# Turning a graph's mask rows with DMA transposes instead of TensorE products

## The chip, the core and the metric

The kernel runs on one core of a Trainium2 chip. The metric is the time of one execution on the device in microseconds (us). The engines are named as in the profile: PE is TensorE (PEld its weight loads), DVE is VectorE, ACT is ScalarE, POOL is GpSimd, SP is SyncE. An engine works through its own list of instructions in order, and that list is fixed when the kernel is built. DMAs are issued from the lists of SP, ACT and POOL.

## The reference

Four graph layers run one behind the other on x (2708 x 512, f32), all with the same 0/1 neighbour matrix adj (2708 x 2708, int32; symmetric pattern with the diagonal set, some 2% ones). Only the first two concern us; layers 2 and 3 are attention layers, which use the same mask.

```python
# layer 0: at most the first 64 neighbours of each row are kept
Ab   = A > 0
keep = Ab & (cumsum(Ab, axis=1) <= 64)
cnt  = keep.sum(axis=1, keepdims=True)
xj   = leaky_relu((keep @ X / max(cnt, 1)) @ W_nb.T + b_nb)
xi   = leaky_relu(X @ W_line.T + b_line)
x    = layernorm(x + xi + where(cnt > 0, xj, 0))
# layer 1: all neighbours
agg  = (adj > 0) @ x / max(deg, 1)
comb = concat([x @ W_self + b_self, agg @ W_nb + b_nb])
x    = layernorm(x + relu(comb @ W_comb + b_comb))
```

## The kernel before

**Tiles.** The 2708 rows are 22 tiles (`NT`) of 128 rows (`P`); the last has 20 (`few`). `maskT` holds the turned mask in SBUF for the whole kernel, one byte an element: `maskT[p, j, n]` belongs to neighbour `j * 128 + p` of row `n`. A neighbour that is among the first 64 has another sign in it than one that comes later, so that layer 0 gets its mask with a Relu of the negated value, and layer 1 by asking for what isn't zero.

**How one mask tile is made.** `turns` lists the tiles in the order in which the mask is made: 20, 21, then 0 to 19; "mask i" below is the i-th of this list. Four steps belong to each.

- `load_mask` (L272): one DMA on POOL's queue reads 128 rows of adj and converts int32 to bf16 on the way into a tile `m` (or `spare`, `w`).
- `count` (L277): ACT turns the row into 0/1 and adds up the degree.
- `place` (L283, L286): DVE runs a scan along the row, which numbers the neighbours, and multiplies the row with it, in two parts (stage 1) or four (stage 2). After this the sign of an element tells whether it is kept.
- `turn` (L295, L299, L302): 22 PE products with an identity write the 128 x 128 blocks turned into PSUM, eight blocks to a bank; ACT's Sign brings each bank to `maskT` as fp8; a small DMA on POOL's queue makes a second copy of the last 20 neighbours' rows on partitions 32 to 51.

**Stage 1 (to about 207 us).** A loop over the 22 tiles of x. For each: `xTs` turns the next x tile on PE (L133, L135); one product with W_nb (L259), whose result `keep_y` stores as a high part by ACT (`yH`, L231) and a low part by DVE (`yL`, L236); one product with W_line (L259), to which DVE adds the bias (`u`, L352) and applies the leaky function (L195); POOL stores that to `r0_dram` (L354). SP loads the x rows (L173) into three buffers, two tiles ahead. The first 14 masks (`HERE`) are made between these steps, at most one per tile: at tile 2, 3 and so on, with two tiles on the way left without one. A mask is turned two tiles after it was counted (one for the last), and there are three buffers `m`, so one mask is loaded while one is counted and placed and one waits for its turn.

**Stage 2 (207 to about 479 us).** `keep @ (X W_nb.T)` for six blocks of up to four row tiles, the blocks in the order of `turns`: for each block, 22 steps over neighbour tiles `j`. A step makes `kT` from maskT on ACT (L369) and runs up to eight matmuls (L496), a high and a low part for each of four row tiles. Each step also asks a generator `both` for one piece of other work: first `other_masks` (masks 14 to 21, in buffers `spare` and `w` by turns), then `weights1` (products of layer 1's weight matrices, one of which it leaves in `weight2`), then `vectors` (24 steps on DVE, L479 and L480, with a load each). What is left of the 132 steps' worth is done at the end. `finish` (L414 to L421) ends layer 0 for the block before. The pools of stage 1 and stage 2 (`l0a`, `l0b`) lie on the same memory, so that stage 2's buffers become free when stage 1's are no longer read.

**Order.** `pe` chains PE's instructions of stage 1 by hand, in the order of the program. `tc.issue_after(ins)` puts the instructions of a block behind `ins` on its engine. Everything else is ordered by the framework's planner when the kernel is built: it goes by the order of the program and by its own estimate of when an instruction's inputs are there, and it waits for a buffer until all uses of the old content are done.

Of the kernel before, what the change touches and what calls it, by code (L numbers as in the profile page):

```python
# [11 lines left out]
BF16 = mybir.dt.bfloat16  # L12
F8 = mybir.dt.float8e4
AF = mybir.ActivationFunctionType
# [4 lines left out]
P = 128  # L19
# [7 lines left out]
STEP = 2.0 ** 68  # L27
# [3 lines left out]
def kernel(  # L31
# [9 lines left out]
    nc = tc.nc  # L41
    N = x.shape[0]
    NT = -(-N // P)
    FULL = N // P
# [5 lines left out]
    def rows(t):  # L50
        return min(P, N - t * P)
# [11 lines left out]
    identb = const.tile([P, P], BF16, name="identb")  # L63
    nc.vector.tensor_copy(identb, ident)
    G = 8
# [16 lines left out]
    maskT = big.tile([P, NT, NT * P], F8, name="maskT")  # L82
# [12 lines left out]
    few = N - (NT - 1) * P  # L95
    LAST, TWIN = NT - 1, 32
# [61 lines left out]
    def early(first, n, make):  # L158

        made = {}  # L160

        def get(i, **how):
            for j in range(len(made), min(i + first + 1, n)):
                made[j] = make(j, **how)
            return made[i]
        return get
# [36 lines left out]
    with ExitStack() as phase:  # L203
        yp = phase.enter_context(tc.tile_pool(name="y", bufs=1))
        cnts = yp.tile([P, NT], F32, name="cnts")
# [3 lines left out]
        gate = yp.tile([P, 1], F32, name="gate")  # L209
        nc.vector.memset(gate, -STEP / 2)  # L210
        weight2 = yp.tile([P, KD, D], F32, name="weight2")
# [6 lines left out]
        ps_mm = phase.enter_context(tc.tile_pool(name="ps_mm", bufs=1, space=PSUM))  # L218
        ps_a = phase.enter_context(tc.tile_pool(name="ps_a", bufs=4, space=PSUM))
        sums = lambda dtype=F32, shape=(P, D): ps_a.tile(list(shape), dtype, name="acc", tag="acc")  # L220
# [44 lines left out]
        HERE = NT - 8  # L265
        cuts = [(b, min(b + 4, NT)) for b in range(0, NT, 4)]
        cuts = cuts[-1:] + cuts[:-1]
        turns = [t for b in cuts for t in range(*b)]

        def load_mask(i, m):  # L270
            n = rows(turns[i])
            nc.gpsimd.dma_start(m[:n], adj[turns[i] * P:turns[i] * P + n, :], max_dma_last_dim=N * 2)  # L272
            return m

        def count(i, m):
            t, n = turns[i], rows(turns[i])
            nc.scalar.activation(m[:n], m[:n], AF.Sigmoid, bias=gate[:n], scale=STEP, accum_out=cnts[:n, t:t + 1])  # L277

        def place(i, m, places, part, of):

            n = rows(turns[i])
            c0, c1 = N * part // of, N * (part + 1) // of
            nc.vector.tensor_tensor_scan(places[:n, :c1 - c0], m[:n, c0:c1], over[:n].to_broadcast([n, c1 - c0]),  # L283
                                         places[:n, c0 - N * (part - 1) // of - 1:][:, :1] if part else -KEEP - 0.5,
                                         OP.add, OP.min)
            return nc.vector.tensor_mul(m[:n, c0:c1], m[:n, c0:c1], places[:n, :c1 - c0])  # L286

        def turn(i, m, psum, order=as_it_comes):
            t, n = turns[i], rows(turns[i])
            for g0 in range(0, NT, G):  # L290
                g1 = min(g0 + G, NT)
                ps = psum()
                for j in range(g0, g1):
                    w = rows(j)
                    order(nc.tensor.transpose(ps[:w, j - g0, :n], m[:n, j * P:j * P + w], identb[:n, :n]))  # L295
                parts = [(P, g0, min(g1, FULL))] + ([(rows(FULL), FULL, NT)] if g1 > FULL else [])
                for w, a, b in parts:
                    if a < b:
                        nc.scalar.activation(maskT[:w, a:b, t * P:t * P + n], ps[:w, a - g0:b - g0, :n], AF.Sign,  # L299
                                             saturate=False)  # L300
                if g1 == NT:
                    nc.gpsimd.dma_start(maskT[TWIN:TWIN + few, LAST, t * P:t * P + n],  # L302
                                        maskT[:few, LAST, t * P:t * P + n])
                yield

        def rows_of(src):
            return early(2, NT, lambda t: fetched(src, t, rows(t)))

        with ExitStack() as ph:
            st = ph.enter_context(tc.tile_pool(name="l0a", bufs=1))  # L310
            wnT, wlT = weight(), weight2
            room = [maskT[:, G + k, :4 * D].bitcast(F32) for k in range(2 * KD)]

            xs = rows_of(x)
            xTs = early(0, NT, lambda t, order=as_it_comes: transposed(ahead, ps_tr, xs(t), rows(t), "xT", order))

            transpose_weight(room[:KD], ps_tr, wnT, l0_w_nb, (nc.sync, nc.scalar))
            lows = {}  # L320
            for t in range(2):
                xT = xTs(t, order=pe)
                lows[t] = keep_y(t, P, product(xT, P, wnT, 0, pe))
            transpose_weight(room[KD:], ps_tr, wlT, l0_w_line)
            b_line = bias(bcast(l0_b_line, D))
            masks = early(1, HERE, lambda i: load_mask(i, st.tile([P, N], BF16, name="m", bufs=3)))
            masks(0)
            nc.gpsimd.memset(maskT[:, NT - 1, :], 0.0)
            nc.gpsimd.memset(maskT[:, :, N:], 0.0)
            counted = turned = 0  # L330
            for t in range(NT):
                n = rows(t)
                if t > 1:

                    lows[t] = keep_y(t, n, product(xTs(t, order=pe), n, wnT, 0, pe, sums() if t % 2 else None))
                xT = xTs(t)
                if t + 1 < NT:
                    xTs(t + 1, order=pe)
                while turned < counted - (t + 2 < NT):
                    for _ in turn(turned, masks(turned), lambda: sums(BF16, (P, G, P)), pe):  # L340
                        pass
                    turned += 1
                now = counted < min(HERE, -(-(t - 1) * HERE // (NT - 5)))
                if now:
                    m, places = masks(counted), st.tile([P, N // 2], BF16, name="places", bufs=1)
                    with tc.issue_after(highs[t].ins):
                        count(counted, m)
                    with tc.issue_after(lows[t].ins):
                        place(counted, m, places, 0, 2)
                pm = product(xT, n, wlT, 1, pe)  # L350
                u = sm.tile([P, D], F32, name="u")
                nc.vector.tensor_add(u[:n], pm[:n], b_line[:n])  # L352
                low = rows_made = leaky(u[:n], u[:n])
                nc.gpsimd.dma_start(r0_dram[t * P:t * P + n, :], u[:n])  # L354
                if now:
                    with tc.issue_after(low.ins):
                        place(counted, m, places, 1, 2)
                    counted += 1
# [3 lines left out]
        with ExitStack() as ph:  # L362
            st = ph.enter_context(tc.tile_pool(name="l0b", bufs=1))
# [8 lines left out]
            def other_masks():  # L372

                def room(i):
                    r = (ahead.tile([P, 2 * KD * (D + 2 * H)], BF16, name="w", tag="w", bufs=1) if i % 2 else
                         st.tile([P, 2 * KD * D], BF16, name="spare", tag="spare"))
                    m = r[:, :N]
                    load_mask(i, m)
                    return m, r[:, N:N + N // 4 + 1]

                got = {HERE: room(HERE)}
                for i in range(HERE, NT):
                    if i + 1 < NT:
                        got[i + 1] = room(i + 1)
                    m, places = got.pop(i)
                    if i == HERE:
                        for _ in range(5):
                            yield
                    count(i, m)
                    yield  # L390
                    yield
                    for part in range(4):
                        place(i, m, places, part, 4)
                        yield
                    yield
                    yield
                    psum = (ps_mm.tile([P, G, P], BF16, name=f"pm{k % 2}") for k in range(3))
                    for _ in turn(i, m, lambda: next(psum)):
                        yield
                nc.vector.tensor_scalar(iso, cnts, 0.5, None, op0=OP.is_lt)  # L400
                nc.vector.tensor_scalar(rdeg, cnts, 1.0, None, op0=OP.max)
                nc.vector.reciprocal(rdeg, rdeg)
# [83 lines left out]
            for i, b in enumerate(cuts):  # L486
# [19 lines left out]
                for t in ts_:  # L506
                    n = rows(t)
# [9 lines left out]
            for t in range(NT):  # L517
                n = rows(t)
# [3 lines left out]
                for p in {19: (16, 17), 20: (18, 19), 21: (20, 21)}.get(t, (t - 3,)):  # L522
                    if p >= 0:
                        with tc.issue_after(low.ins):
                            nc.vector.tensor_scalar(maskT[:, p, :], maskT[:, p, :], 0.0, None, op0=OP.not_equal,
                                                    saturate=False)
                if t + 1 < NT:
                    xTs(t + 1)
                pm = product(xT, n, wself, 1)
# [4 lines left out]
        with ExitStack() as ph:  # L534
            st = ph.enter_context(tc.tile_pool(name="l1b", bufs=2))
            for t in range(NT):
                n = rows(t)
# [3 lines left out]
                for g0 in range(0, NT, G):  # L541
                    g1 = min(g0 + G, NT)
# [948 lines left out]
```

## Time and profile before

| | |
|---|---|
| median of 3 runs | 2942.97 us (2942.67 to 2946.18) |
| profiled execution | 2939.28 us, span 2937.5 us, mean granted clock 0.995 |
| PE, DVE, ACT, POOL busy | 97%, 68%, 52%, 7% of the span |
| products with the identity (L295) | 308 in stage 1, 176 in stage 2 |
| Sign from PSUM to maskT (L299) | 56 instructions in stage 1, 32 in stage 2; 1.03 us at the longest |
| loads of mask rows (L272) | 14 in stage 1, 8 in stage 2 |

Lines of the profile give the line of the kernel, the engine, the operation, what it writes and reads, its shapes and how often it occurs; in brackets how long the engine was idle just before, and for whom. In the timeline the first two columns are the start and the time of a group of like instructions, in us. "pm", "acc" and "ps_tr" are PSUM buffers. Numbers at the end of names are left out, so `weight` in the profile is `weight2`.

### The profile page before, as it was taken

The page shows a single profiled execution, that of the slowest core. Times are in us where ns is not written, and L with a number is a line of the kernel's source. Part 1 is how long each engine was busy: PE and PEld are TensorE (multiplying, and loading weights), DVE is VectorE, ACT ScalarE, POOL GpSimd, SP SyncE. Part 2 cuts the span into 40 slices and gives each one's busy share as a digit, 9 for nine tenths or more (in the row PEclk, how much of TensorE's full clock was granted, in tenths as well). Part 3 has the DMA queues.
Part 4 walks back from the last instruction along what each step waited for, and adds up shares of the span by engine and source line. Part 5 has one row for each costly group of instructions (what it writes and reads, how often), then busy time and mean ns, then how long its engine had stood idle before and what let it go on. Part 6 is the DMA issues. An engine that isn't in the chain of part 4 may idle for free. (4 is left out here: it accounts for less than half of the span.)

```text
span 2937.5 us, 36437 instructions
## 1 busy us (share of the span) xinstructions
PE 2854.5 (97%) x14354; PEld 1590.3 (54%) x14354; DVE 1996.9 (68%) x2409; ACT 1515.0 (52%) x1761; POOL 220.2 (7%) x375
## 2 busy tenths in 40 slices
PE   8999999999999999999999999999999999999997
PEld 4557766458887333444466433444475555555555
DVE  6866637443234999999977999999953435445242
ACT  3546532123323999999965999999951000000001
POOL 1111101101110000000022000000000000000000
PEclk9999999999999999999999999999999999999999
DMA  5633326322222011111143111121061000000000
GB/s 131 129 87 76 104 79 192 113 67 91 81 74 82 30 40 39 38 45 48 32 151 123 40 40 39 43 64 37 33 158 61 4 26 15 25 15 16 15 22 21
DMA packets 121886, 185.71 MB, mean 63 GB/s; under 512 B 42455, under 2 KB 67276, under 8 KB 121706
## 3 DMA queue, kind: packets, MB, share of 16 engines
q1 hardware_dynamic: 91838, 121.62, 13.8%
q0 software_dynamic: 18864, 57.45, 6.9%
q10 hardware_dynamic: 11004, 4.22, 0.6%
q8 instruction: 115, 1.88, 0.3%
q14 instruction: 65, 0.53, 0.1%
HBM read 153.10 MB, written 44.65 MB: 67 GB/s over the span
## 5 line engine op out<-in xcount | busy, mean ns | idle before, releaser
L743 DVE SCALAR_TENSOR_TENSOR e<-v_bc,ucol,maskT 128x1408 f32<-128x1408 f32 (+3 forms) x804 | 1135.9, 1468 | 326.9 <-PE pn L1119 313.4
L770 ACT ACTIVATE c<-e,bcol 128x1300 fp8e4<-128x1300 f32 (+1 forms) x688 | 965.5, 1422 | 65.3 <-DVE e L743 22.3
L937 PE MATMUL po<-e,R 128*64 128x512 f32 (+2 forms) x4224 | 907.5, 549 | 30.4 <-DVE e L743 27.4
L937 PEld LDWEIGHTS po<-e,R 128*64 128x64 f32 x4224 | 341.9, 137 | 563.0 <-issue 386.1
L1119 PE MATMUL pn<-e,R 128*128 128x512 f32 (+3 forms) x1056 | 403.0, 545 | 1.1 <-DVE lin L1139 0.3
L1119 PEld LDWEIGHTS pn<-e,R 128*128 128x128 f32 (+1 forms) x1056 | 183.9, 190 | 197.1 <-issue 181.5
L1069 ACT ACTIVATE w<-pl,b 128x256 f32<-128x256 f32 (+1 forms) x88 | 41.0, 466 | 371.2 <-PE pl L1067 371.2
L496 PE MATMUL acc<-yH,kT 128*128 128x512 f32 x484 | 195.2, 409 | 4.6 <-ACT kT L369 4.5
L547 PE MATMUL acc<-yH,mf 128*128 128x512 f32 x484 | 185.0, 389 | 0.0
L496 PE MATMUL acc<-yL,kT 128*128 128x512 f32 x462 | 180.7, 391 | 0.0
L547 PE MATMUL acc<-yL,mf 128*128 128x512 f32 x462 | 179.7, 389 | 0.0
L663 PE MATMUL pm<-w,xT 128*128 128x264 f32 (+1 forms) x704 | 165.3, 387 | 2.0 <-ACT xT L135 1.1
L259 PE MATMUL pm<-weight,xT 128*128 128x512 f32 (+1 forms) x344 | 158.4, 603 | 8.1 <-DVE u L352 6.8
L1067 PE MATMUL pl<-lin 128*128 128x256 f32 (+1 forms) x704 | 156.1, 376 | 3.4 <-DVE lin L966 3.4
L122 POOL TENSOR_TENSOR ln_rs<-ln_rs,half 128x1 f32<-128x1 f32 (+1 forms) x88 | 53.5, 608 | 1407.7 <-DVE ln_rs L121 1358.2
L1092 PE MATMUL pl<-lin,w 128*128 128x512 f32 x336 | 150.8, 593 | 0.0
L1067 PEld LDWEIGHTS pl<-lin 128*128 128x128 f32 x704 | 131.3, 193 | 34.6 <-issue 15.8
L544 ACT CAST mf<-maskT 128x1024 fp32r<-128x1024 fp8e4 (+1 forms) x66 | 64.5, 978 | 151.7 <-PE acc L547 148.1
L663 PEld LDWEIGHTS pm<-w,xT 128*128 128x128 f32 (+1 forms) x704 | 127.9, 187 | 26.2 <-issue 2.9
L259 PE MATMUL pm<-w,xT 128*128 128x512 f32 x296 | 133.6, 594 | 5.3 <-ACT xT L135 2.1
L369 ACT ACTIVATE kT<-maskT 128x512 fp32r<-128x512 fp8e4 (+1 forms) x132 | 77.5, 594 | 115.5 <-PE acc L496 114.3
L839 PE MATMUL pd<-c,parts_c 128*12 128x384 fp8e4 (+2 forms) x2752 | 128.3, 307 | 0.0
(247 smaller groups left out, 2643.2 us busy)
## 6 DMA issues: line engine op xcount, KB each, us to landing
rows<-x_dram SPq DMA_DIRECT2D x63, 256.0 KB
v_bc<-v_dram SPq DMA_DIRECT2D x16, 704.0 KB
rows<-in_x_dram SPq DMA_DIRECT2D x42, 256.0 KB
x_dram<-u POOLq DMA_DIRECT2D x42, 256.0 KB, 2.6
v_bc<-v_dram SPq DMA_DIRECT2D x16, 650.0 KB
m<-in_adj_dram POOLq DMA_DIRECT2D x13, 677.0 KB, 7.0
r_dram<-u POOLq DMA_DIRECT2D x21, 256.0 KB, 2.4
rows<-r_dram SPq DMA_DIRECT2D x21, 256.0 KB
```

The lines of the kernel that those rows point to most:

```text
L259: order(nc.tensor.matmul(pm[:m], xT[:, k, :m], w[:, k, :], start=(k == 0), stop=(k == KD - 1)))
L369: made = nc.scalar.activation(kT[:, :w], maskT[:, j, b[0] * P:b[0] * P + w], AF.Relu, scale=-1.0)
L496: nc.tensor.matmul(pa[t], kT[:, (t - b[0]) * P:(t - b[0] + 1) * P], y[:, j, :], start=(j == 0 and y is yH), stop=(j == LAST))
L547: nc.tensor.matmul(pa, mf[:, j - g0, :], y[:, j, :], start=(j == 0 and y is yH), stop=(j == LAST))
L663: nc.tensor.matmul(pm[a][:m, :D // 2 + heads], xT[:, k, :m], w[:, k, a, :D // 2 + heads], start=(k == 0), stop=(k == KD - 1))
L743: self.made = nc.vector.scalar_tensor_tensor(e[:, :w], v[:, :w], ucol[:, j, h:h + 1], maskT[:, j, c0:c0 + w], op0=OP.max, op1=OP.mult)
L770: nc.scalar.activation(c[:, :w], e[:, :w], AF.Sigmoid, bias=bcol[:, j, h:h + 1], scale=STEP, saturate=False)
L839: pe(nc.tensor.matmul(p[32 * g:32 * g + 12, :c1 - c0], parts_c[:, j, h, :], c[:, c0:c1], start=(i == 0 and h == hs[0]), stop=(i == NT - 1 ...
L937: pe(nc.tensor.matmul(po[i][HO * k:HO * k + HO, :c1 - c0], R2[:, j, h * HO:(h + 1) * HO], e[:, c0:c1], start=(i_ == 0), stop=(i_ == NT - 1)))
L1067: nc.tensor.matmul(pl[:, :w], self.lin1[:, k, f * P:(f + 1) * P], h[:, k, :w], start=(k == 0), stop=(k == KD - 1))
L1092: nc.tensor.matmul(pl[:n], gT[:, f, (t - t0) * P:(t - t0) * P + n], self.lin2[:, f, :], start=(f == 0), stop=(f == KF - 1))
L1119: nc.tensor.matmul(pn[k][:, :w], R2[at, j, k * P:(k + 1) * P], e[at, :w], start=(j == 0), stop=(j == NT - 1))
```

## The change

The 22 products and the PSUM buffers are gone. `turn` is one DMA transpose on SP's queue from the mask tile into a bf16 tile of the turned shape (`turned_` in stage 1, the memory of `weight2` in stage 2). A new generator `signs` has ACT bring that tile to `maskT` in four instructions of 8, 8, 5 and 1 blocks, and then issues the small second copy. `signs` of a mask runs just before the next mask is turned (stage 1), or between the four parts of the next mask's `place` (stage 2).

As the transpose takes whole blocks of 128, a mask tile has 2816 columns instead of 2708; POOL clears the last 108 before each load, and the whole tile where it has only 20 rows. In stage 1 there are two buffers `m` instead of three, besides the one `turned_`. Each mask of stage 2 takes as many steps of `both` as before, and the signs of the last one four more.

```diff
         def load_mask(i, m):
...
-            nc.gpsimd.dma_start(m[:n], adj[turns[i] * P:turns[i] * P + n, :], max_dma_last_dim=N * 2)
+            nc.gpsimd.dma_start(m[:n, :N], adj[turns[i] * P:turns[i] * P + n, :], max_dma_last_dim=N * 2)
...
-        def turn(i, m, psum, order=as_it_comes):
+        def turn(i, m, into):
+            nc.sync.dma_start_transpose(into, m)
+
+        def signs(i, into):
             t, n = turns[i], rows(turns[i])
-            for g0 in range(0, NT, G):
-                g1 = min(g0 + G, NT)
-                ps = psum()
-                for j in range(g0, g1):
-                    w = rows(j)
-                    order(nc.tensor.transpose(ps[:w, j - g0, :n], m[:n, j * P:j * P + w], identb[:n, :n]))
-                parts = [(P, g0, min(g1, FULL))] + ([(rows(FULL), FULL, NT)] if g1 > FULL else [])
-                for w, a, b in parts:
-                    if a < b:
-                        nc.scalar.activation(maskT[:w, a:b, t * P:t * P + n], ps[:w, a - g0:b - g0, :n], AF.Sign,
-                                             saturate=False)
-                if g1 == NT:
-                    nc.gpsimd.dma_start(maskT[TWIN:TWIN + few, LAST, t * P:t * P + n],
-                                        maskT[:few, LAST, t * P:t * P + n])
+            for w, a, b in [(P, a, min(a + G, FULL)) for a in range(0, FULL, G)] + [(few, FULL, NT)]:
+                nc.scalar.activation(maskT[:w, a:b, t * P:t * P + n], into[:w, a:b, :n], AF.Sign, saturate=False)
                 yield
+            nc.gpsimd.dma_start(maskT[TWIN:TWIN + few, LAST, t * P:t * P + n],
+                                maskT[:few, LAST, t * P:t * P + n])
...
-            masks = early(1, HERE, lambda i: load_mask(i, st.tile([P, N], BF16, name="m", bufs=3)))
+            turned_ = st.tile([P, NT, P], BF16, name="turned", bufs=1)
+
+            def mask_rows(i):
+                m = st.tile([P, NT * P], BF16, name="m", bufs=2)
+                nc.gpsimd.memset(m[:, N:], 0.0)
+                if rows(turns[i]) < P:
+                    nc.gpsimd.memset(m, 0.0)
+                return load_mask(i, m)
+
+            masks = early(1, HERE, mask_rows)
...
                 while turned < counted - (t + 2 < NT):
-                    for _ in turn(turned, masks(turned), lambda: sums(BF16, (P, G, P)), pe):
+                    for _ in signs(turned - 1, turned_) if turned else ():
                         pass
+                    turn(turned, masks(turned), turned_)
                     turned += 1
+                if t + 1 == NT:
+                    for _ in signs(turned - 1, turned_):
+                        pass
...
                 def room(i):
...
-                    m = r[:, :N]
+                    m = r[:, :NT * P]
+                    nc.gpsimd.memset(m[:, N:], 0.0)
                     load_mask(i, m)
...
+                into = weight2.rearrange("p k c -> p (k c)").bitcast(BF16)[:, :NT * P].rearrange("p (t n) -> p t n", n=P)
                 for i in range(HERE, NT):
...
                     for part in range(4):
                         place(i, m, places, part, 4)
+                        next(left, None)
                         yield
+                    for _ in left:
+                        pass
                     yield
                     yield
-                    psum = (ps_mm.tile([P, G, P], BF16, name=f"pm{k % 2}") for k in range(3))
-                    for _ in turn(i, m, lambda: next(psum)):
-                        yield
+                    turn(i, m, into)
+                    left = signs(i, into)
+                    yield
+                    yield
+                    yield
+                for _ in left:
+                    yield
```

More of the change, by code (lines that the diff above doesn't have):

```diff
@@ L276, in count @@
             t, n = turns[i], rows(turns[i])
-            nc.scalar.activation(m[:n], m[:n], AF.Sigmoid, bias=gate[:n], scale=STEP, accum_out=cnts[:n, t:t + 1])
+            nc.scalar.activation(m[:n, :N], m[:n, :N], AF.Sigmoid, bias=gate[:n], scale=STEP, accum_out=cnts[:n, t:t + 1])
         def place(i, m, places, part, of):
@@ L376, in room @@
                          st.tile([P, 2 * KD * D], BF16, name="spare", tag="spare"))
-                    m = r[:, :N]
+                    m = r[:, :NT * P]
+                    nc.gpsimd.memset(m[:, N:], 0.0)
                     load_mask(i, m)
-                    return m, r[:, N:N + N // 4 + 1]
-                got = {HERE: room(HERE)}
+                    return m, r[:, NT * P:NT * P + N // 4 + 1]
+                got, left = {HERE: room(HERE)}, iter(())
+                into = weight2.rearrange("p k c -> p (k c)").bitcast(BF16)[:, :NT * P].rearrange("p (t n) -> p t n", n=P)
                 for i in range(HERE, NT):
```

## The prediction

> **What bounds the kernel now.** I read the page first, then the busy times by stretch, then the answer on the products of the old turning (L295), then the timeline of stage 1, then the DMA issues.
>
> ```profile
> span 2937.5 us, 36437 instructions
> PE 2854.5 (97%) x14354; PEld 1590.3 (54%) x14354; DVE 1996.9 (68%) x2409; ACT 1515.0 (52%) x1761; POOL 220.2 (7%) x375
> ```
>
> TensorE is busy 97% of the span, so work taken off it should count, but only where it ends last. The stretches (PE, PEld, DVE, ACT, POOL busy, then clock, DMA share, GB/s) show two kinds of place.
>
> ```profile
> 100.00:150.00 50.00, 48.14 (x204) 24.90 (x203) 45.90 (x43) 28.61 (x40) 8.38 (x14) 1.00 0.60 123
> ...
> 300.00:350.00 50.00, 49.45 (x248) 38.26 (x247) 38.10 (x55) 28.02 (x43) 7.93 (x12) 1.00 0.40 101
> ```
>
> In stage 1 (to 207 us) DVE is nearly as full as PE; in stage 2 (300 to 350) PE alone is the bound. The old turning is in both:
>
> ```profile
> L295 PE MATMUL acc<-identb,m x308: 166/219/230, 50.3 to 195.3; 128*128 128x128 bf16 x143, 20*128 20x20 bf16 x11
> ...
> L295 PE MATMUL pm<-identb,w x88: 219/219/232, 232.4 to 376.1; 128*128 128x128 bf16 x84, 128*20 128x128 bf16 x4
> ```
>
> 308 products turn 14 masks in stage 1; in stage 2 twice 88 (the line shown and its like for the tile spare) turn 8. A product's 219 ns is mostly pipeline: the timeline has 22 begin at 159.03 and the next matmul at 160.45, so 1.42 us a mask, 65 ns a product. One mask in steady state, the lines of masks before and behind it left out:
>
> ```profile
> 117.91 0.72 POOL L272 DMA_DIRECT2D m<-in_adj_dram  x1
> ...
> 125.06 2.55 ACT L277 ACTIVATE m<-m,gate 128x2708 bf16<-128x2708 bf16 x1 [0.43 <-DMA m<-in_adj_dram]
> ...
> 130.97 2.97 DVE L283 TENSOR_TENSOR_SCAN places<-m,over 128x1354 bf16<-128x1354 bf16 x1
> ...
> 139.15 0.86 DVE L286 TENSOR_TENSOR m<-m,places 128x1354 bf16<-128x1354 bf16 x1
> ```
>
> The mask is loaded (7.15 us from issue to use), counted, and placed from 130.97 to 140.0, 9.0 us with three small DVE instructions inside; PE's next product, at 125.93, waits 0.66 us for DVE's u (L352). The next mask's scan comes 9.56 us after this one's: that pace is DVE's, not PE's, whose turn costs 8.83 us with a mask and 7.3 without. The ends of stage 1, and what idling costs PE:
>
> ```profile
> 57.03 0.84 DVE L286 TENSOR_TENSOR m<-m,places 20x1354 bf16<-20x1354 bf16 x1
> ...
> 62.65 5.37 PE L259 MATMUL pm<-weight,xT 128*128 128x512 f32 x8 [2.11 <-DVE u L352]
> ...
> 182.96 0.86 DVE L286 TENSOR_TENSOR m<-m,places 128x1354 bf16<-128x1354 bf16 x1
> ...
> 206.89 0.50 PE L496 MATMUL acc<-yH,kT 128*128 128x512 f32 x1
> ```
>
> Mask 1 is placed at 57.9, mask 13 at 183.8, stage 2 runs from 206.9 (two of its matmuls, 0.5 us, came earlier, so 206.4). The eight matmuls behind a 2.1 us idle took 5.37 instead of 3.70.
>
> Last, prices of transfers, issue to landing in us:
>
> ```profile
> m<-in_adj_dram POOLq DMA_DIRECT2D x13, 677.0 KB, 7.0
> ...
> oT_dram<-oT POOLq DMA_DIRECT2D x4, 704.0 KB, 3.6
> ```
>
> **Part by part.**
>
> *Stage 2, products gone.* 176 x 65 ns = 11.5 us off the engine that bounds it. ACT's signs have the shapes of the old evacuations (1.03, 1.03, 0.72, 0.25 us), read SBUF instead of PSUM, and are taken at the same cost. A mask takes 11 steps as before, about 1.88 us each (eight matmuls 0.235 apart), so the three steps behind the turn and the two behind the count leave some 9 us before the first sign: they hide a DMA up to 9 us. Without that cover ACT would wait with kT behind it and PE behind kT. **-11.5**.
>
> *Stage 1, products gone.* 14 x 1.42 = 20 us of PE, but with masks arriving at DVE's pace most of it only turns into waiting for DVE. It is not counted by itself: the chain below decides the end.
>
> *Two mask buffers instead of three, and the buffer held until the DMA has read it.* This is the new wait. The load of mask i+2 (and the memset before it, on POOL) waits until the transpose of mask i has landed; that waits on SP for mask i's last product with places. So from "mask i placed" to "mask i+2 placed": transpose T, memset 0.3 (128x48 took 0.14, 128x128 f32 0.20, plus hand-over), load 7.0, count 2.7, place 9.0, hand-over to SP 0.2: 19.2 + T. Before, a third buffer covered the load. Queued behind the waiting memset on POOL is a store of r0, whose u tile (two buffers) DVE then needs; behind the waiting transpose on SP are loads of x rows, two tiles ahead; behind a waiting count on ACT the yH copies. Loads now start up to 2.1 us after their buffer is free (117.91 against 115.83, behind such a store); here that would count. Bounds 0 and 2.1 a pair; I take 0.5, as it arises only when the store's turn falls badly.
>
> *T.* The trace has no transpose. It moves 128 x 2816 x 2 B = 704 KB. A plain move of 704 KB lands in 3.6; the mask load, which handles every element since it converts, lands in 7.0 (6.5 to 12.5). A transpose also handles every element, so I take **6**, nearer the latter, and keep 3.6 and 12.5 as ends.
>
> One rule speaks against the change: the Trainium skill, "VectorE: DVE Perf Modes", section "The three transpose paths", lists 390 ns for a 128x128 bf16 transpose on TensorE and 1309 on the DMA, and its "Rules for kernel authors" prefer TensorE where PSUM will do as destination. The 65 ns measured here for one of a row of 22 is far below the page's 390, so that figure overprices what is removed; 22 x 1309 ns would by estimate make T 28.8 and the sum some 160 us larger. The skill's "DMA: Bandwidth & Descriptors", section "Latency and other measured facts", gives 261 GB/s for DMA transposes: by estimate T 2.8, and the sum about -15.
>
> *Sum for stage 1.* Pair: 19.2 + 6 + 0.5 = 25.7. Mask 13 is six pairs behind mask 1: 57.9 + 154.2 = 212.1. Then its transpose 6, signs 2.7, first kT 0.4: 221.2. Stage 2 can't begin before: its buffers lie on those of stage 1 (now mask 14's load waits for mask 13's last product). Products of the x tiles don't depend on masks and should run ahead, done near 206.4 - 20 = 186. So stage 2 starts 14.8 later; PE, idle before, begins slowly, +1.7 (5.37 - 3.70). **+16.5**.
>
> *Tail of stage 2.* other_masks now yields 97 steps, not 93 (four signs of the last mask), so of all 140 the 132 in the blocks leave four more vector steps to the end: 4 x (0.69 + 0.69) = 5.5 us of DVE around 480 to 500, where DVE is full and PE waited 0.4. Between 0 and 5.5; I take **+2**, since only what holds back a yL or u costs.
>
> *Rest.* The full memset of the short mask falls before 10 us and is needed at 42.5: nothing; uncovered it would cost about 2.5 (a memset of 2816 fp8).
>
> Total: -11.5 + 16.5 + 2 = **+7** on the profiled 2939.28 (span 2937.5), 2946.3; the median 2942.97 is 3.7 above that run, so **2950.0**. Each us of T counts seven times: +7 + 7 x (T - 6).
>
> **Rivals.**
>
> *Cheap transpose.* T = 3.6 as the plain move: 7 - 16.8 = -9.8, so 2933. For: same bytes, and the DMA engines are 0.60 busy in the fullest stretch. Against: per-element work. The sign turns at T = 5. A still shorter T gains less and less, as DVE's own work (9.56 a mask) takes over: what can go there are its gaps around the two tiles without a mask, some 6 us, and the 1.4 of turning at tile 20, so stage 1 -7.5, in all about -17, 2926.
>
> *Products don't run ahead.* If queue order keeps tiles 19 to 21 behind mask 13, the 22.6 us from last place to stage 2, less 1.4, come after 212.1: 233.3, +26.9 instead of +14.8, without the slow start: -11.5 + 26.9 + 2 = +17.4, 2960. For: DVE and ACT work in order, counts now wait for loads. Against: the trace has u (L352) set between scan and product where that was ready.
>
> *Long transpose.* Contended as the slowest mask load was: T = 12.5, +52.5, 2995. For: the same 0.60, and POOL's loads, stores and the transposes meet. Against: median 7.0. That the transposes aren't single transfers but fall into small pieces would look the same.
>
> **How the numbers follow.** Forecast 0.34 (T 5 to 7: 2943 to 2957), cheap 0.30, not ahead 0.20, long 0.16. A measurement can tell about 0.2% (5.9 us) from no change. Forecast: 0.14 within, 0.20 slower. Cheap: 0.26 faster, 0.04 within. The others are slower. Faster 0.26, same 0.18, slower 0.56. The range goes from 2926 to 2985 (T near 11), leaving out some of long and what may lie below cheap. Since both signs hold much, the forecast's own range is 2943 to 2957.
>
> **What would show it.** Right: no L295 products; 22 SP transposes landing near 6 us; from mask 2 on, scans in stage 1 some 12.8 us apart; POOL's memset waiting for the transpose; first L496 near 221; PE in stage 2 shorter by 11.5. Wrong: landing under 5 us with scans near 9.6 apart and an earlier stage 2; matmuls of tiles 19 to 21 behind mask 13's place; ACT waiting for the transposes in stage 2 with kT behind, which would give back the 11.5.

## The result: 2955.2 us, 0.4% slower

The changed kernel takes 2955.19 us in the median of 6 runs (2954.36 to 2958.68), the kernel before 2943.66 in the same series (2940.78 to 2946.18): ratio 1.004, 95% interval 1.0027 to 1.0053. The profiled execution took 2954.36 us. The page:

```profile
span 2952.5 us, 35575 instructions
PE 2833.2 (96%) x13870; PEld 1568.3 (53%) x13870; DVE 1997.9 (68%) x2409; ACT 1522.1 (52%) x1761; POOL 261.1 (9%) x398
```

PE has 484 instructions and 21 us of work less than before, and the span is 15.0 us longer. The stretches shown before (PE, PEld, DVE, ACT, POOL busy, clock, DMA share, GB/s):

```profile
100.00:150.00 50.00, 39.43 (x100) 17.83 (x99) 38.93 (x34) 25.85 (x32) 8.55 (x17) 0.92 0.82 166
300.00:350.00 50.00, 48.28 (x205) 37.36 (x205) 40.09 (x63) 31.42 (x48) 10.39 (x17) 1.00 0.62 145
```

In stage 1 PE falls from 48.1 of 50 us to 39.4 and DVE from 45.9 to 38.9: now no engine is full there, so a wait sets the end. In stage 2 (second line) PE is still nearly full. The instructions of the new turning line (L289; min/median/max in ns, first and last start) and who waits for them:

```profile
L289 SPq DMA_TRANSPOSE turned<-m x14: 3283/3386/5587, 50.6 to 214.2; - x14
L289 SPq DMA_TRANSPOSE weight<-spare x4: 3289/3318/3369, 250.9 to 371.1; - x4
...
  POOL m L323: 70.5, 12
  ACT maskT L294: 41.7, 15
```

The 3.4 us (the median) are the time for which a transpose holds SP's list: after the one at 150.53 the next load on SP is issued at 154.00. POOL's memset (L323), and with it the load of the next mask, waits 70.5 us in 12 waits. One cycle of a mask, other lines left out:

```profile
132.28 0.72 POOL L272 DMA_DIRECT2D m<-in_adj_dram  x1 [0.29 <-issue]
...
138.94 2.55 ACT L277 ACTIVATE m<-m,gate 128x2708 bf16<-128x2708 bf16 x1 [4.40 <-DMA m<-in_adj_dram]
...
141.62 2.98 DVE L283 TENSOR_TENSOR_SCAN places<-m,over 128x1354 bf16<-128x1354 bf16 x1 [3.86 <-ACT m L277]
...
149.52 0.85 DVE L286 TENSOR_TENSOR m<-m,places 128x1354 bf16<-128x1354 bf16 x1
...
150.53 3.38 SPq L289 DMA_TRANSPOSE turned<-m  x1
...
157.13 0.19 POOL L323 MEMSET m<- 128x108 bf16 x1 [5.28 <-DMA turned<-m]
```

Load 6.66 us, count 2.68, place 8.75, hand-over 0.16, landing 6.60: 24.85 from the load until the same buffer is cleared again. Two buffers take turns at that, so a mask comes every 12.6 us (mean of the first scans from 66.55 to 205.30) where it was 9.56. The ends of stage 1:

```profile
58.97 0.84 DVE L286 TENSOR_TENSOR m<-m,places 20x1354 bf16<-20x1354 bf16 x1
...
205.30 2.98 DVE L283 TENSOR_TENSOR_SCAN places<-m,over 128x1354 bf16<-128x1354 bf16 x1 [4.04 <-ACT m L277]
...
209.69 3.03 DVE L283 TENSOR_TENSOR_SCAN places<-m,places,over 128x1354 bf16<-128x1354 bf16 x1
...
212.63 0.67 DVE L358 TENSOR_TENSOR u<-pm,bias 128x512 f32<-128x512 f32 x1
213.22 0.85 DVE L286 TENSOR_TENSOR m<-m,places 128x1354 bf16<-128x1354 bf16 x1
...
213.35 3.70 PE L259 MATMUL pm<-weight,xT 128*128 128x512 f32 x8 [1.25 <-DVE u L358]
...
220.77 3.70 PE L259 MATMUL pm<-weight,xT 128*128 128x512 f32 x8
...
226.14 3.64 PE L259 MATMUL acc<-w,xT 128*52 128x512 f32 x8 [1.67 <-POOL xT L257]
...
233.94 0.50 PE L511 MATMUL acc<-yH,kT 128*128 128x512 f32 x1
```

Mask 13 is placed at 214.07. One of PE's eight-matmul products began 0.7 us earlier (213.35), behind u; four more, those of the last two tiles, come only then, and stage 2 starts at 233.94, 27.05 us later than before (206.89). What PE and ACT waited for in stage 1 (us in total, times, longest):

```profile
ACT m L277 <- DMA m<-in_adj_dram: 44.2, 11, 5.5
...
ACT maskT L294 <- DMA turned<-m: 39.6, 14, 8.9
...
PE pm L259 <- DVE u L358: 30.0, 12, 5.7
```

ACT waits 84 us in all for loads and landings, with copies to yH and xT behind these waits in its list; PE waits 30.0 us for u, which before was 5.5.

### The profile page after: what moved, and what is told of

It reads as the page before. It is cut to its first block, busy times and chain, and to the rows that moved or that the text cites. A ratio compares the mean times of both kernels' runs of the same rounds, so it can differ in the third digit from the quotient of the medians.

```text
span 2952.5 us, 35575 instructions
## 1 busy us (share of the span) xinstructions
PE 2833.2 (96%) x13870; PEld 1568.3 (53%) x13870; DVE 1997.9 (68%) x2409; ACT 1522.1 (52%) x1761; POOL 261.1 (9%) x398
## 2 busy tenths in 40 slices
DMA packets 184538, 201.50 MB, mean 68 GB/s; under 512 B 105111, under 2 KB 129932, under 8 KB 184362
## 5 line engine op out<-in xcount | busy, mean ns | idle before, releaser
L1084 ACT ACTIVATE w<-pl,b 128x256 f32<-128x256 f32 (+1 forms) x88 | 41.1, 467 | 369.8 <-PE pl L1082 369.8
L259 PE MATMUL pm<-weight,xT 128*128 128x512 f32 (+1 forms) x344 | 166.3, 629 | 32.1 <-DVE u L358 31.3
```

The source lines that it names most:

```text
L259: order(nc.tensor.matmul(pm[:m], xT[:, k, :m], w[:, k, :], start=(k == 0), stop=(k == KD - 1)))
```

## Experiments

The kernel before took 2941 to 2946 us (medians of 15 to 19 runs) beside these. "Stage 1 ends" below is PE's first matmul of stage 2 in the profile, 202.66 before and 229.71 after (two such matmuls come some 4 us ahead of the rest). These ends have some 2 us of play: the first mask's scan starts at 39.2 to 39.5 us in five of the fourteen profiles (39.30 before) and at 41.1 to 41.8 in nine (41.25 after), whatever was edited.

**The change in stage 2 alone** (stage 1 with three buffers and products as before)

```diff
-                    for _ in signs(turned - 1, turned_) if turned else ():
+                    for _ in turn_pe(turned, masks(turned), lambda: sums(BF16, (P, G, P)), pe):
                         pass
-                    turn(turned, masks(turned), turned_)
...
```

> DMA transposes for the eight masks of stage 2 alone; stage 1 with products and three buffers as in the kernel before. Theory, buffers: stage 2 loses 176 products of 65 ns and nothing waits for the transposes: stage 2 takes 261 us instead of 272.4, the start of layer 1 is 1.4 us shorter as well, time about 2943.7 - 12.8 = 2931 us. Rival, traffic: transposes cost what they bring also here (signs that come late hold kT); time 2940 us or more.

Measured: 2933.23 us, ratio 0.9961 (0.9949 to 0.9973), 11.5 below the kernel before in that series. Stage 1, unchanged, ends at 204.30 in this profile. The eight landings cost next to nothing: PE's idle time for kT is 6.5 us, 4.5 before. The transpose issued at 225.46 clears the way for the next memset at 230.86, 5.4 us later, and five steps of PE's work, some 9 us, hide it.

**The change in stage 1 alone**

```diff
-                    turn(i, m, into)
-                    left = signs(i, into)
-                    yield
-                    yield
-                    yield
+                    psum = (ps_mm.tile([P, G, P], BF16, name=f"pm{k % 2}") for k in range(3))
+                    for _ in turn_pe(i, m, lambda: next(psum)):
+                        yield
```

> DMA transposes for the 14 masks of stage 1 alone, two buffers; stage 2 with products as in the kernel before. Theory, buffers: the whole loss and none of the gain: stage 2 starts near 234 and takes 272 us, time about 2955 + 12.8 = 2968 us. Rival, that part of the loss comes from stage 2 (late masks, more steps at its end): 2960 us or less.

Measured: 2969.61 us, ratio 1.0091 (1.0077 to 1.0105), +24.9; stage 1 ends at 229.60, as with the whole change. The two halves add up: +24.9 and -11.5 make +13.4, the whole is +11.5. All of the loss comes with the change in stage 1.

**Each transpose of stage 1 twice**

```diff
-            nc.sync.dma_start_transpose(into, m)
+            for _ in range(2 if i < HERE else 1):
+                nc.sync.dma_start_transpose(into, m)
```

> Each transpose of stage 1 is issued twice in a row, the same content to the same place; the rest is the changed kernel (2955.2 us). If the time from place to landing (T, 6.5 us) is a term of the chain that sets stage 1, a second transpose lengthens it by at least the 3.4 us for which one held SP, at most by another 6.5: six pairs of masks and the last one make 7 x 3.4 = +24 to 7 x 6.5 = +45, so 2979 to 3000 us. If stage 1 is set by something else (the order of the products, the missing buffer without regard to T), the second transpose fills a queue that otherwise idles: under +8, below 2963 us.

Measured: 3018.36 us, ratio 1.0241 (1.0221 to 1.0261), some 60 us above the changed kernel, with stage 1 ending at 290.98. More than expected, and the profile says why (SP's list, then POOL's):

```profile
115.16 12.28 SPq L290 DMA_TRANSPOSE turned<-m  x2
```

```profile
129.43 0.19 POOL L324 MEMSET m<- 128x108 bf16 x1 [12.98 <-DMA turned<-m]
```

The second transpose writes the same tile as the first and goes 8 to 10 us after it (one pair at 96.42 and 106.13), so a dose is a whole landing, not SP's 3.4 us: from issue to the memset 14.3 us in this pair. From the end of place to the memset it is 16.3 us in the mean of 12 masks, 6.7 in the changed kernel. A pair of masks took 36.0 us instead of 25.2: 9.6 us more landing make 10.8 more per pair. So T is a term of the chain, with a factor of about one per pair, as the prediction's sum had it. The products of the last tiles are done by 248.4 here, while mask 13 is placed only at 277.05: the chain alone sets this end.

**A third mask buffer** (on memory of yL that is written last)

```diff
-                m = st.tile([P, NT * P], BF16, name="m", bufs=2)
+                m = (yp.tile([P, NT * P], BF16, name="m3", tag="late") if i % 3 == 2 else
+                     st.tile([P, NT * P], BF16, name="m", bufs=2))
```

> The changed kernel with three mask buffers in stage 1 (the third on memory that stage 1's low parts need only from tile 18 on). Theory, buffers: the pace of 12.6 us a mask comes from the load of mask i+2 waiting for the transpose of mask i (pair 19.2 + 0.5 + 6 us); a third buffer covers it, so scans come 9.6 us apart as before, stage 2 starts near 206 and the time is about 2955 - 27 = 2928 us. Rival, traffic: the transposes crowd the DMA engines (0.77 busy in stage 1 against 0.51) and slow loads and stores however many buffers there are; then scans stay 12 us or more apart and the time stays above 2948 us.

Measured: 2942.53 us, ratio 0.9991 (0.9981 to 1.0). Between the two theories. Stage 1 ends at 216.21: of stage 1's 27 us the buffer gives 13.5 back. The first masks come 9 to 10 us apart as before, then there are holes (ACT's and PE's lines of the timeline):

```profile
93.92 2.83 ACT L304 ACTIVATE maskT<-turned 128x1024 fp8e4<-128x1024 bf16 x4 [10.88 <-DMA turned<-m]
...
97.74 5.40 PE L269 MATMUL acc<-w,xT 128*128 128x512 f32 x8 [4.30 <-ACT xT L135]
```

This mask's transpose was issued at 82.06, held SP for 7.02 us and landed only after 11.9 (the DMA engines were 0.88 busy from 50 to 90 us, 0.82 in the changed kernel's 100 to 150); ACT's signs waited for it with the next copy to xT behind them. From issue to the memset it is 7.9 us in the mean of 11 masks, 6.6 in the changed kernel. So the missing buffer was half of stage 1's loss, and with it back the landing itself took longer.

**Products ahead: 11 masks in the loop, three after it**

```diff
...
-                now = counted < min(HERE, -(-(t - 1) * HERE // (NT - 5)))
+                now = counted < min(11, -(-(t - 1) * 11 // (NT - 5)))
...
+            while turned < HERE:
+                if counted < HERE:
+                    m, places = masks(counted), st.tile([P, N // 2], BF16, name="places", bufs=1)
+                    count(counted, m)
...
+                turn(turned, masks(turned), turned_)
```

> The changed kernel with 11 masks between the x tiles instead of 14 and the last three after them, so that products of tiles 19 to 21 needn't stand behind mask 13 in the queues. Theory, queue order: two things make stage 1 longer, the pace of the masks (12.6 us) and the three tiles behind the last one (19.9 us from its place to stage 2); here only the first is left, mask 13 is placed near 213 as in the changed kernel, stage 2 starts near 225 instead of 234 and the time is about 2946 us. Rival, pace alone: the planner would have held the products back anyway, stage 2 starts within 3 us of 234, time 2952 to 2958 us.

Measured: 2960.67 us, ratio 1.0054 (1.0042 to 1.0066), missed by both. The products are done by 219, and then:

```profile
225.99 3.75 SPq L289 DMA_TRANSPOSE turned<-m  x1
...
235.02 0.79 PE L521 MATMUL acc<-yH,kT 128*128 128x512 f32 x1 [15.93 <-ACT kT L385]
```

Stage 2 now follows the last transpose by 9.0 us, the 9.1 of the prediction's sum, but that transpose starts at 226.0 instead of 214.2: the first scans come 13.8 us apart in the mean (64.69 to 216.40) where they came 12.6. In the program a mask is counted and placed behind the copies of its x tile, which would make tiles without a mask hold the chain up as masks hold the products; that reading of the 13.8 is argued, not shown. What is shown is that the products, put ahead, leave the masks later.

**Cut transposes** (10 and 12 blocks, the first after the first part of place)

```diff
-            nc.sync.dma_start_transpose(into, m)
+            for a, b in ((0, 10), (10, NT)) if i < HERE else ((0, NT),):
+                nc.sync.dma_start_transpose(into[:, a:b], m[:, a * P:b * P])
```

> Each transpose of stage 1 is cut in two, blocks 0 to 9 and 10 to 21; the first may go after the first part of place, 3.9 us (a scan of 3.0 and a product of 0.85) before the second part is done. The same bytes move, and there are still two buffers. If T is a term of the chain, what follows the second part is 12 of 22 blocks: T falls from 6.5 us to between 3.6 (in proportion) and 4.5, which in six pairs and the last mask is 7 x 2.0 to 7 x 2.9, -14 to -20 us: 2935 to 2941 us. If the traffic of the transposes or the order of the products sets stage 1, nothing comes back: 2952 to 2960 us.

Measured: 2958.24 us, ratio 1.0036 (1.0024 to 1.0049). The premise was half wrong: from the end of place to the memset the mean fell from 6.7 to 5.4 us only (12 masks each). Even these 1.4 us a pair did not arrive, as a pair took 25.5 us (25.2 in the changed kernel), and the time lies in the second theory's range. ACT's waits for landings rose from 39.6 to 62.7 us.

**ACT's order: signs behind the copy of the next x tile** (`copies[0]` is ACT's last copy to xT), with two buffers, and the same with cut transposes

```diff
-                    for _ in signs(turned - 1, turned_) if turned else ():
-                        pass
+                    with tc.issue_after(copies[0].ins):
+                        for _ in signs(turned - 1, turned_) if turned else ():
+                            pass
```

> The changed kernel with its two mask buffers (2955.2 us); only the order of ACT's list is another: in stage 1 the signs of a mask stand behind the copy of the next x tile. If the chain through the two buffers (load, count, place, landing) sets stage 1, ACT's order is beside it: 2951 to 2957 us. If it was ACT's waiting for landings, 39.6 us in 14 waits with copies and counts behind them, that held the products, up to 10 us come back: about 2945 us.

> The transposes of stage 1 cut in two, with two buffers, and the signs behind the copy of the next x tile. Cut alone they gave 2958.2 us, though the place-to-landing time of the second half was 3.8 us in the trace instead of 6.5; ACT then waited 62.7 us in 18 waits for landings, since the signs of the first half came earlier in its list. If that waiting ate the gain, this one has it: 7 x 2.7 = 19 us below 2955, about 2937 us. If a shorter landing gives nothing because DVE and ACT are shared by masks and products (one list each), it stays at 2952 to 2958 us.

Measured: 2968.65 us, ratio 1.0078 (1.0064 to 1.0092); cut as well 2975.94, 1.0101 (1.0085 to 1.0117). Neither theory of either run had slower. The same transfers and buffers, and 11 us more if each is taken against the kernel before in its own series (+22.5 and +11.5). In the profiles stage 1 ends 8.4 us later, at 238.08. The profile of the first:

```profile
110.19 2.55 ACT L277 ACTIVATE m<-m,gate 128x2708 bf16<-128x2708 bf16 x1 [15.38 <-DMA m<-in_adj_dram]
112.74 0.56 ACT L231 CAST yH<-acc 128x512 fp32r<-128x512 f32 x1
...
113.20 0.58 ACT L135 COPY xT<-ps_tr 128x512 f32<-128x512 f32 x1
...
113.84 5.40 PE L259 MATMUL pm<-w,xT 128*128 128x512 f32 x8 [4.51 <-ACT xT L135]
```

A count that waits for its load stands ahead of yH and xT, as in the changed kernel, but here it waits up to 15.4 us, there up to 5.5. ACT waited 64.4 us for loads (44.2 in the changed kernel), and PE 26.6 us for xT (7.1 there). So a product also waits for whatever wait of the mask chain stands ahead of its copy in ACT's list. Mask 13 is placed at 228.31, 14.2 us later, but most of the last products are then done, and stage 2 follows 9.8 us behind it. Why the masks came so much later was not taken apart. The question whether a shorter landing helps is not settled by the second run, since this order masks it.

**Three buffers with late signs, and with cut transposes too**: the edits above together.

> The kernel with a third mask buffer (2942.5 us), and in stage 1 the signs of a mask stand behind ACT's copy of the next x tile instead of before it. With the third buffer ACT waited for landings 62.9 us in 14 waits, the longest 10.9, with that copy behind it, and PE then 4.3 us. If this order of ACT's list is what the third buffer left, PE's waits for xT and for what follows from it go, some 10 us: about 2932 us. If it is the landing itself, which took 9 to 12 us in that run while the DMA engines were 0.9 busy, the masks still wait for it: 2940 to 2945 us.

> Third buffer, late signs and cut transposes together. If all three act on the chain of masks, the scans come at the pace of the kernel before (9.6 us) and PE, with 308 products fewer in stage 1, ends that stage before 207 us: 2920 to 2932 us. If the DMA engines' traffic is the limit, cutting does nothing and the time is that of late signs with the third buffer, within 3 us.

Measured: 2939.55 us, ratio 0.9981 (0.997 to 0.9992), and 2945.28, 0.9991 (0.9981 to 1.0001). Stage 1 ends at 218.04 and 213.71 in the profiles. The scan of mask 13 begins at 188.5 and 184.1, with the third buffer alone at 189.0: late signs take ACT's waits for landings from 62.9 to 4.1 and 5.3 us and PE's for xT from 7.3 to 5.1 and 2.4, but bring the masks hardly earlier. The eight runs of the first reach from 2937 to 2948 and the ten of the second from 2938 to 2948, and the profiled one was the slowest of the eight and nearly the fastest of the ten. That is wider than what separates the three-buffer kernels, so neither these times nor these profiles rank them.

**Even masks by DMA, odd ones by products**, three buffers, late signs

```diff
+                    if turned % 2:
+                        for _ in turn_pe(turned, masks(turned), lambda: sums(BF16, (P, G, P)), pe):
+                            pass
+                    else:
...
-                    turn(turned, masks(turned), turned_)
+                        turn(turned, masks(turned), turned_)
```

> Third mask buffer and late signs; of the 14 masks of stage 1 the even ones are turned by the DMA transpose, the odd ones by 22 products each as before the change; stage 2 by DMA transposes. So 154 of 308 products are back, and half of the transposes' traffic in stage 1 is gone. If the landings (6 to 11 us with every mask) were what slowed the third buffer's masks, every second mask frees its buffer early, the scans come about 9.6 us apart as before the change, and PE has 154 x 65 ns = 10 us less to do than there: 2933 (transposes in stage 2 alone) less 10, about 2923 us. If one landing per two masks still holds the chain, stage 1 is as with late signs and the third buffer: 2938 to 2945 us.

Measured: 2938.52 us, ratio 0.9976 (0.9967 to 0.9985); stage 1 ends at 208.40. SP was held 3.3 to 3.5 us per transpose, ACT waited 13.0 us for loads and 3.1 for landings, and still stage 1 ended 5.7 us later than before the change (the first scan 2.2 us later), with 10 us of products gone. The stretch 60 to 110:

```profile
60.00:110.00 50.00, 48.73 (x185) 24.03 (x184) 47.10 (x44) 27.85 (x40) 10.42 (x21) 0.97 0.70 155
```

DVE (third pair) is busy 47.1 of 50 us, and 91.9 of 100 up to 160; before the change 91.3. This fits DVE as what decides where the landing no longer does; PE's saved products did not shorten stage 1.

**The same with 12 masks in stage 1 instead of 14** (against the kernel just above)

```diff
-        HERE = NT - 8
+        HERE = NT - 10
...
-                m = (yp.tile([P, NT * P], BF16, name="m3", tag="late") if i % 3 == 2 else
+                m = (yp.tile([P, NT * P], BF16, name="m3", tag="late") if i % 3 == 0 else
...
                     for _ in left:
                         pass
-                    yield
-                    yield
                     turn(i, m, into)
```

> As the kernel that turns even masks by DMA and odd ones by products (2938.5 us), but with 12 masks in stage 1 and 10 in stage 2, each mask of stage 2 taking 9 steps instead of 11. In that kernel SP's transposes were out of the way (3.4 us each), PE had 10 us less to do in stage 1 and still ended it later than before the change; DVE was busy 92 of 100 us from 60 to 160. If DVE's work on masks and tiles (two scans and two products, 7.75 us a mask, and 2.05 us a tile) is what then holds stage 1, two masks fewer give 2 x 7.75 = 15.5 us, and stage 2, where DVE is busy about 60% of the time, hides them: about 2923 us. If the order of the lists holds it, with a place between every two products, only the 22 products of the one odd mask leave (1.4 us): 2935 to 2939 us. If stage 2 cannot hide two more masks, it is above 2940 us.

Measured: 2935.62 us, ratio 0.9981 (0.9971 to 0.999). Stage 1 ends at 196.81, 11.6 us earlier for 15.5 us of DVE's work; the order of the lists alone was to give 1.4, so this fits DVE as what held stage 1 with 14, though each mask takes its other steps along. From 60 to 160 us DVE is now busy 83.6 of 100 and PE 94.4. Against the kernel before in its own series the total did not move (0.9981 after 0.9976), because stage 2 gives it back:

```profile
L543 PE MATMUL acc<-yH,kT 128*128 128x512 f32 x484 | 195.7, 410 | 14.4 <-ACT kT L409 11.4 <-ACT u L556 3.0
```

PE's idle time ahead of these matmuls is 14.4 us; with 14 masks in stage 1 it was 8.4. From the end of stage 1 to the end of the span it is 2735.0 us, against 2728.3 with 14 masks.

**All spans together.** Span less the end of stage 1 is 2734.8 us before the change and 2738.2 in the kernel with the change in stage 1 alone; in the eleven others, with transposes in stage 2 and eight masks there, it lies from 2722.8 (the changed kernel) to 2729.2. So the end of stage 1 carries nearly all of the larger differences between these kernels. Small ones can't be read from single profiles: from the turn of the last x tile in layer 1's projection to the end, where no edit reaches, the fourteen profiles lie between 2304.8 and 2312.0 us.

**The best version** is the change in stage 2 alone, 2933.2 us, below both kernels. No version with transposes in stage 1 came below it; the intervals of the last two, with half of stage 1's masks turned by products, overlap with its own.

## Why the number was near, and which step was not right

Direction and range held: +0.4% where slower had the most chance, 2955.2 against 2950.0. The working behind it did not hold throughout, and that the number came so near is in part luck: between the spans the change cost 15.0 us, nearer to the rival's 17.4 than to the forecast's 7.

- *Stage 2, -11.5.* Between PE's first matmul of stage 2 proper and the layer-1 projection the trace has 260.99 us (233.94 to 494.93) against 272.39: -11.40. Alone it measured -11.5. The 65 ns a product, taken from a row of 22, was the right price here, and the cover of 9 us held: PE's idle time for kT rose only from 4.5 to 6.4 us.
- *The chain, 25.7 a pair.* 25.2 measured from mask 2 on, with T 6.7 instead of 6 and the load 6.5 instead of 7.0, so neither rival on T (3.6 and 12.5) came true. That T would lie above the plain move's 3.6 held; that this comes from handling every element, as the prediction argued, no run shows. From mask 1's place (59.81) to mask 13's (214.07) it is 154.3 us, the sum's 154.2; mask 13 came 2.0 us after 212.1 because mask 1 came 1.9 late, with the later first scan. The doubled transposes show T as a term of the chain.
- *The step that failed: "Products of the x tiles don't depend on masks and should run ahead, done near 206.4 - 20 = 186."* By data they don't depend; in the lists of ACT and DVE they stand between counts and places. The u at 212.63 adds the bias to a product of PE that was done at 204.3 (200.58 and 3.70 us). DVE then idled until 205.30 for mask 13's count, and u came only behind both scans of that mask, with PE's product at 213.35 waiting for it. PE was idle for 37 of the 164 us from 50 to 214, so there was room for them. The products of the last two tiles came behind mask 13's place, so from there to stage 2 it took 19.9 us and not 9.1, and stage 1 lost 27.05 us instead of 16.5. The +1.7 for a slow start of PE did not come, as products kept it at work up to stage 2. This is the rival "products don't run ahead", whose 233.3 for stage 2's start was 0.6 us off. Before the change these products followed mask 13 too (183.8 to 206.9); that was in the trace and was read as PE's being full. That the lists hold the products is shown by this wait and by the kernel with products ahead, where they were done by 219.1 and stage 2 followed mask 13's place by 9.4 us; with the signs late it followed by 9.8. But mask 13 itself then came 11.6 and 14.2 us later, so neither order reached the prediction's 221.2.
- *Tail, +2.* The difference against the kernel before falls from 15.65 us at the layer-1 projection to 14.26 after it: -1.4.
- *The sum.* Stage 1 was 10.55 too low (the products 10.8 and the later start 2.0, less 1.7 for PE's slow start and the 0.5 of early matmuls that the sum took off 206.9), the tail 3.4 too high, and what follows layer 1's projection added 0.7: +15.0 in the spans against +7. Of that error the medians show only 5.2, since the profiled run of before lay 3.7 under its median and that of after 0.8 under its own.

A rule that spoke against the change can now be weighed. The transpose of 22 blocks landed in 5.3 to 6.1 us in stage 2 and 6.7 in stage 1 (mean of 12, from the end of place). By the Trainium skill, "VectorE: DVE Perf Modes", section "The three transpose paths", 22 blocks at 1309 ns would by estimate take 28.8 us; the measured landings are far below that, so the figure does not add up block by block. The prediction's other estimate, 2.8 us, was too low. The advice to turn on TensorE agreed with the runs in stage 1, but for another reason than the page's figures, the buffer held and the lists blocked; it did not agree in stage 2, where TensorE was the bound.

What stays open: how much of the remaining 11 to 15 us of the three-buffer kernels (up to 2 of them from the start) is the longer landing under traffic and how much is DVE. The traffic of stage 1 was not taken away by itself.

## What to carry to other kernels

Moving work from the engine that is full to a DMA paid where the result is needed later than it lands and nobody's list stands behind it, in stage 2; the same edit cost 24.9 us in stage 1, where the buffer was on a loop of load, work and landing. When a buffer count falls, write the loop per buffer and its period first. And before you let independent work "run ahead", read in the trace in which list it stands and behind which wait: an in-order list makes a dependency that the data doesn't have.

## What was not expected of the hardware

- A DMA transpose of 704 KB held the queue that issued it for 3.3 to 3.4 us at the least, and up to 7.7 us in the kernel with the third buffer (at 154.35, the DMA engines 0.94 busy from 150 to 165); the x rows on SP were issued only behind it. A plain load of x rows on the same queue held it for 0.37 us in the median (0.29 to 1.27).
- The transposes fall into small pieces: packets under 512 bytes rose from 42455 to 105111 in the span, and the DMA share in 100 to 150 us from 0.60 to 0.82 at 166 GB/s instead of 123.
- Eight matmuls in a row that mostly take 3.6 to 3.7 us took 5.1 to 6.4 in five of 17 cases behind an idle time of PE in stage 1 (at 206.27, 5.40 after 1.99; but at 161.18, 3.70 after 2.52). The granted clock there was 0.92 in 100 to 150, where it had been 1.00.
